# Channel attention as one pipeline of 36 pieces, with the next image's statistics in the scan

## The chip, the cores and the metric

The kernel runs on one core of a Trainium2 chip. Its time is the device time of one execution in microseconds (us), the median of three runs. The engines are TensorE (PE, with its weight loads as PEld), VectorE (DVE), ScalarE (ACT), GpSimd (POOL) and SyncE (SP), which issues the DMAs. All data are float32.

## The reference

Eight images of 384 channels and 64x64 pixels go through two layers, each added to its input. Layer 0 is attention over channels, layer 1 a selective scan over the pixels in four directions.

```python
x = x + conv_attention(gn(x))          # layer 0
x = x + selective_scan(gn(x))          # layer 1

gn(v): 32 groups of 12 channels; (v - mean) / sqrt(var + 1e-5) over group and pixels

conv_attention(x):
    q, k, v = [dwconv3x3(conv1x1(x, w), dw) for w, dw in ((wq, dwq), (wk, dwk), (wv, dwv))]
    q, k, v = split into 8 heads of 48 channels, each [48, 4096]
    q, k = q / |q|, k / |k|            # over the 4096 pixels
    attn = softmax(q @ k.T * temperature)          # [48, 48] a head
    return conv1x1(attn @ v, wproj)

selective_scan(x): for 4 orders of the 4096 pixels (rows, columns, both reversed)
    dt, B, C = projections of x        # per pixel: 384, 16 and 16 values
    for each pixel: h = h * exp(dt * A) + (dt * x) * B;  y = sum(h * C over 16) + D * x
    y of the 4 orders is summed; layer norm over channels; gelu
```

## The kernel before

Channels lie on partitions, as three blocks (`NJ`) of 128; an image is three tiles of 128x4096. Images go one after the other: `channel_attention(b)`, then `selective_scan(b)`. The finish of image b (layer norm, gelu, the addition, the store) is done within the attention of image b+1, and for the last image by `finish` at the end. Most order in the scan is pinned by `keep_in_program_order` (`pin`); the instructions of the attention were placed by a scheduler, from the order in which they are written.

*Attention.* `norm_factors` turns statistics (`bn_stats`, L162; `bn_aggr`, L118) into mean and inverse deviation of each group, with small matmuls against `avg` (L126, L138) and a Sqrt on ACT (L143). `weights` scales a 384x384 weight with it (L197) and makes the bias that replaces the mean (L201, L206). `conv` makes one block of 128 channels of k, q or v: 512 pixels at a time go through three matmuls (L226) into PSUM and with the bias on ACT into `pre` (L231). The 3x3 depthwise convolution follows: the centre tap is an ACT product (L236) or, with the taps above and below, three matmuls with diagonal weights (L249, copied by ACT at L254); all other taps are DVE operations `out = pre * w + out` (L266), over up to 64 rows each. `to_tokens` transposes k and q by PE (L290) with ACT copies (L291), `inverse_norm` squares and sums on ACT (L277), and L327 multiplies q and k over pixels. Masked softmax follows on DVE and ACT (L332 to L344), its result is multiplied into `wproj` (L362), and `project_out` applies that to v (L375), adds it to x (L380), takes the statistics for the second layer (L381) and stores x1. k and q go block by block over all rows, v in three stripes of rows. `token_norm` (L815, L816) takes the layer norm statistics of the last image at the start; `emit` places its 16 finish parts between the parts of v (L831, L838, L839, L843).

*Scan.* The second normalisation is applied in place (L438 on ACT for 6 of 24 blocks, L443 on DVE). Then 32 steps (4 orders by 8 chunks of 512 pixels) of 12 units (3 channel blocks by 4 groups of 4 states). A unit has four DVE scans (L586) of 512 pixels, four exponentials on ACT (L562), one POOL product of 128x2048 (L574), 16 PE transposes (L607), four ACT copies (L613) and 32 small products (L624). A step also has `step_size` (L528, L536, Softplus, with two table loads), `weigh` (L545), the layout of C (`mingle_c` on POOL L496, `turn_c` on PE L502, `spread_c` on DVE L513), and the loads of B (`fetch`, L519) from DRAM, where `lay_out` stored them. Results leave PSUM by DVE (L664, L666) and are added up in DRAM. In the last step `load_x` loads the next image into the tiles of x, and its 24 `bn_stats` blocks follow: one a unit after unit 5, and the rest behind the last scan.

All DMAs are issued by SP, in order. [...]

## Time and profile before

| | us |
|---|---|
| median of three runs | 19907.61 |
| lowest and highest | 19904.44, 19921.87 |
| the profiled execution's own time | 19929.61 |
| its span in the profile | 19927.8 |
| image 0: start to first scan | 488 |
| image 1: last scan of image 0 to its first scan | 490.4 |
| image 1: first to last scan | 1994.6 |
| last scan of image 7 to the end | 104 |

The mean granted PE clock is 0.949 of full speed. A row of the page gives line, engine, operation, output and inputs, count, busy time, mean duration in ns, and then how long the engine was idle before such instructions and what ended that. In a list in order of time, a row begins with start and length in us; several equal instructions are one row with their count (x8). Two instructions in a row overlap by some 0.1 us, as the next one starts before the last one's end is reported; so prices for a full queue are read from start to start. A float32 matmul is two instructions in this profile.

### The profile page before, as it was taken

The page shows a single profiled execution, that of the slowest core. Times are in us where ns is not written, and L with a number is a line of the kernel's source. Part 1 is how long each engine was busy: PE and PEld are TensorE (multiplying, and loading weights), DVE is VectorE, ACT ScalarE, POOL GpSimd, SP SyncE. Part 2 cuts the span into 40 slices and gives each one's busy share as a digit, 9 for nine tenths or more (in the row PEclk, how much of TensorE's full clock was granted, in tenths as well). Part 3 has the DMA queues.
Part 4 walks back from the last instruction along what each step waited for, and adds up shares of the span by engine and source line. Part 5 has one row for each costly group of instructions (what it writes and reads, how often), then busy time and mean ns, then how long its engine had stood idle before and what let it go on. Part 6 is the DMA issues. An engine that isn't in the chain of part 4 may idle for free. (4 is left out here: it accounts for less than half of the span.)

```text
span 19927.8 us, 414273 instructions
## 1 busy us (share of the span) xinstructions
PE 17323.4 (87%) x167376; PEld 10365.3 (52%) x167376; DVE 18841.2 (95%) x17078; ACT 16772.8 (84%) x29347; POOL 15425.1 (77%) x6798
## 2 busy tenths in 40 slices
PE   7888888888888888888888888888888888888887
PEld 4555545555455554555545555455554555545554
DVE  7999989999899998999989999899998999989998
ACT  3999949999499985999859998599985999859998
POOL 0999909999099980999819998199981999729997
PEclk9999989999899999999999999999999999999998
DMA  1232322323223232232322323223232222322223
GB/s 43 83 96 96 99 81 83 96 96 102 78 83 97 96 106 75 84 95 97 110 75 83 98 97 104 75 86 96 96 104 74 85 96 96 104 74 86 96 96 124
DMA packets 1194155, 1814.00 MB, mean 91 GB/s; under 512 B 153552, under 2 KB 1018064, under 8 KB 1055024
## 3 DMA queue, kind: packets, MB, share of 16 engines
q1 hardware_dynamic: 1191376, 1787.38, 27.5%
q8 instruction: 1321, 21.64, 0.4%
q14 instruction: 594, 4.87, 0.1%
q10 hardware_dynamic: 864, 0.12, 0.0%
HBM read 1468.39 MB, written 318.77 MB: 90 GB/s over the span
## 5 line engine op out<-in xcount | busy, mean ns | idle before, releaser
L574 POOL TENSOR_TENSOR db<-w,B 128x2048 f32<-128x2048 f32 x3072 | 14062.9, 4581 | 640.8 <-DVE h L586 428.9
L586 DVE TENSOR_TENSOR_SCAN h<-da,ca,db 128x512 f32<-128x512 f32 x10752 | 12785.7, 1266 | 285.0 <-ACT da L562 266.1
L562 ACT ACTIVATE da<-dt,neg_a 128x512 f32<-128x512 f32 x12288 | 8757.4, 714 | 156.4 <-DVE h L586 152.6
L607 PE MATMUL pt<-ident,h 128*128 128x128 f32 x49152 | 8091.3, 293 | 736.4 <-DVE h L586 468.7
L613 ACT COPY hc<-pt 128x512 f32<-128x512 f32 x12288 | 7411.5, 605 | 651.1 <-PE pt L607 590.1
L607 PEld LDWEIGHTS pt<-ident,h 128*128 128x128 f32 x49152 | 5420.5, 145 | 3192.8 <-issue 1892.3
L624 PE MATMUL py<-hc,cp 128*32 128x128 f32 x98304 | 5053.6, 289 | 898.6 <-ACT hc L613 726.3
L624 PEld LDWEIGHTS py<-hc,cp 128*32 128x32 f32 x98304 | 2039.4, 109 | 3163.9 <-ACT hc L613 1625.9
L423 POOL MEMSET wdt<- 128x1536 f32 x8 | 11.0, 1378 | 3564.8 <-DMA x1d<-x 3564.8
L586 DVE TENSOR_TENSOR_SCAN h<-da,db 128x512 f32<-128x512 f32 x1536 | 1747.7, 1209 | 83.4 <-ACT da L562 78.8
L474 PE MATMUL px<-x,wx 128*44 128x128 f32 x6144 | 1214.2, 341 | 50.2 <-ACT x L438 28.9
L545 POOL TENSOR_TENSOR w<-x,dt 128x512 f32<-128x512 f32 x744 | 1065.0, 1431 | 22.5 <-ACT dt L536 20.5
L474 PEld LDWEIGHTS px<-x,wx 128*44 128x44 f32 x6144 | 684.3, 127 | 378.6 <-issue 189.0
L528 PE MATMUL pd<-xd,wdt 128*128 128x512 f32 x1536 | 732.7, 613 | 157.9 <-DVE h L586 152.1
L513 DVE TENSOR_TENSOR cp<-quad,pct 128x512 f32<-128x512 f32 x1024 | 630.3, 683 | 44.9 <-PE pct L502 44.9
L375 PE MATMUL pp<-v,mT 128*128 128x512 f32 x1152 | 550.3, 631 | 117.2 <-DVE v L266 57.3
L600 POOL COPY ca<-h 128x4 f32<-128x4 f32 x2688 | 543.0, 202 | 0.0
L536 ACT ACT_TABLE_LOAD x256 | 328.4, 1283 | 229.3 <-PE pd L528 228.3
L528 PEld LDWEIGHTS pd<-xd,wdt 128*128 128x128 f32 x1536 | 272.5, 190 | 466.7 <-issue 238.2
L536 ACT ACTIVATE dt<-pd,dt_bias 128x512 f32<-128x512 f32 x768 | 475.7, 686 | 6.8 <-PE pd L528 2.2
L375 PEld LDWEIGHTS pp<-v,mT 128*128 128x128 f32 x1152 | 227.0, 203 | 394.7 <-issue 309.8
L666 DVE TENSOR_TENSOR ys<-ys,py 128x512 f32<-128x512 f32 x576 | 387.8, 673 | 4.3 <-PE py L624 4.3
(374 smaller groups left out, 10986.2 us busy)
## 6 DMA issues: line engine op xcount, KB each, us to landing
B<-bcd SPq DMA_DIRECT2D x1024, 1024.0 KB, 4.7
yd<-ys SPq DMA_DIRECT2D x384, 256.0 KB, 3.3
ys<-yd SPq DMA_DIRECT2D x768, 128.0 KB, 2.8
yd<-ys SPq DMA_DIRECT2D x768, 128.0 KB, 4.4
x<-in_x SPq DMA_DIRECT2D x48, 1024.0 KB, 5.5
x1d<-x SPq DMA_DIRECT2D x192, 256.0 KB, 2.0
ys<-yd SPq DMA_DIRECT2D x192, 256.0 KB, 2.9
fy<-yd SPq DMA_DIRECT2D x128, 384.0 KB, 3.8
```

Of the source, the lines that this page charges most:

```text
L375: nc.tensor.matmul(pc, lhsT=mT[:, j, bass.ts(m, P)], rhs=v[:, j, bass.ts(c, CH)], start=j == 0, stop=j == NJ - 1,)
L474: pin(nc.tensor.matmul(split(pxs[s][:XR, :])[:, part, :], lhsT=wx[:, j, k, :], rhs=view(x1[j], k, c)[:, part, :], start=i == 0, stop=i == ...
L513: pin(nc.vector.tensor_mul(t, m.broadcast_to([P, NQ, HP]), c.broadcast_to([P, NQ, HP])))
L528: pin(nc.tensor.matmul(pd, lhsT=wdt[:, k, bass.ts(j, P)], rhs=xds[s], start=True, stop=True))
L536: pin(nc.scalar.activation(dts[s, j], pd, AF.Softplus, bias=small["dt_bias"][:, j, k : k + 1]))
L545: pin(eng.tensor_mul(split(ws[s, j]), view(x1[j], k, c), split(dts[s, j])))
L562: pin(nc.scalar.activation(t, dts[s, j], AF.Exp, scale=neg_a[:, j, steps[s][0], n : n + 1]))
L574: pin(eng.tensor_mul(t, w.broadcast_to([P, NV, CH]), bts[s, g]))
L586: pin(nc.vector.tensor_tensor_scan(h, da, db, 0.0 if start else carries[s - 1][:, j, n : n + 1], ALU.mult, ALU.add,))
L607: pin(nc.tensor.transpose(t[:, f, :], hs[u][:, bass.ts(q, HP), :].rearrange("p l v -> p (l v)"), ident))
L613: pin(nc.scalar.copy(t, pts.pop((u, lb))))
L624: pin(nc.tensor.matmul(py[f * HP : (f + 1) * HP, lb, :], lhsT=cps[s, g][:, q, :], rhs=hc[:, f, :], start=g == lb == 0, stop=g == NG - 1 an ...
```

## The change

k, q and v are cut into 36 pieces of 16 rows (`PR`), first k and q block by block, then v with its three blocks in turn, and one loop over the pieces works at four of them at once: in step t, the 1x1 convolution of piece t+2 (`band`), the first products of piece t+1 (`start_sum`, `end_sum`), the closing of piece t (`finish_sum`), and, for k and q, transposes and squares of piece t-1 (`to_tokens`). All is pinned in this order.

The nine taps of a piece are split. ACT makes four products of 1024: one neighbouring row, left, right and centre. POOL adds left and right to the row's product. The centre goes to a PSUM tile of two banks (`ac`), DVE adds the five other taps to it there, and a last DVE addition joins both sums. No tap is a matmul now.

q's products with k, the norms and the softmax become steps of the loop; the roots are exp(-0.5 ln v) with one refinement. From step 27 on, projections and the finish of the last image run beside the pieces of v; its addition moves from DVE to POOL. The last image's layer norm statistics (`last_stats`) are read four parts ahead of the first piece and twelve parts during q.

The statistics of the next image move into the scan: `look_ahead` reads x a second time, in eight chunks of 128x3x512, takes their statistics in steps 29 to 31, and in the last step computes the norm factors, loads and scales the weight of k and makes its bias. At the start of the scan C's layout comes before the first products, ACT normalises three blocks before and nine after the first two decays, DVE twelve. `avg` is loaded once. The pools get `reuse_waits="tile"`.

```diff
+PR = 16
+NP = H // PR
+BR = CH // W
...
-def x_stats(x, stats, blocks):
-    for j, c in blocks:
-        tc.keep_in_program_order(
-            nc.vector.bn_stats(stats[:, j, c, :], x[j][:, bass.ts(c, CH)])
-        )
...
+while loaded:
+    i, y, x = loaded.pop(0)
+    pz = [bank(i, h) for h in range(2)]
+    for j in range(NJ):
+        for t in range(n):
+            pin(nc.tensor.transpose(
+                pz[j // 2][:, bass.ts((j % 2) * n + t, P)],
+                y[:, t * C + j * P : t * C + (j + 1) * P], ident,
+            ))
+    if loaded:
+        even(*loaded[0])
+    yield
+    cs, o = bass.ts(i, FT), y.rearrange("p (j l) -> p j l", l=FT)
+    for j in range(NJ):
+        pin(nc.scalar.activation(
+            o[:, j, :], pz[j // 2][:, (j % 2) * FT : (j % 2 + 1) * FT], AF.Gelu,
+            bias=small["ln_b"][:, j : j + 1], scale=small["ln_w"][:, j : j + 1],
+        ))
+    load_rest()
+    pin(nc.gpsimd.tensor_add(x, y, x))
+    load()
+    nc.sync.dma_start(
+        out_d[b, :, :, cs].rearrange("j p l -> p j l"), x.rearrange("p (j l) -> p j l", l=FT)
+    )
+    yield
...
-for tap in range(9):
-    if tap == 4:
-        continue
-    dy, dx = tap // 3 - 1, tap % 3 - 1
-    r0, r1 = max(y0, -dy), min(y1 if dx else ys, H - dy)
-    if r0 >= r1:
-        continue
-    x0, x1 = max(0, -dx), W - max(0, dx)
-    o = out3[:, r0 - y0 : r1 - y0, x0:x1]
-    nc.vector.scalar_tensor_tensor(
-        o, pre3[:, r0 + dy - lo : r1 + dy - lo, x0 + dx : x1 + dx],
-        dw[:, m, tap : tap + 1], o, ALU.mult, ALU.add,
-    )
...
-parts = (0, H // 2, 3 * H // 4, H)
-todo, left, edges = [], list(range(L // FT)) if emit else [], {}
-for y0, y1 in zip(parts, parts[1:]):
-    for m in range(NJ):
...
-        if m > 0:
-            for _ in range(min(len(todo), 6)):
-                project_out(*todo.pop(0))
-        for _ in range(min(len(left), 2)):
-            emit(left.pop(0))
-    todo += [(m, c) for c in range(y0 * W // CH, y1 * W // CH) for m in range(NJ)]
-for t in todo:
-    project_out(*t)
...
+work = st.enter_context(tc.tile_pool(name=f"a{b}", bufs=2, reuse_waits="tile"))
+ps_c = st.enter_context(tc.tile_pool(name=f"pc{b}", bufs=3, space=PSUM, reuse_waits="tile"))
+ps_s = st.enter_context(tc.tile_pool(name=f"ps{b}", bufs=2, space=PSUM, reuse_waits="tile"))
+ps_a = st.enter_context(tc.tile_pool(name=f"pa{b}", bufs=1, space=PSUM, reuse_waits="tile"))
...
+for j in range(NJ):
+    pin(nc.tensor.matmul(
+        pc[:, : n * W], lhsT=wts["w" + w][:, j, bass.ts(m, P)],
+        rhs=x[j][:, r * W : (r + n) * W], start=j == 0, stop=j == NJ - 1,
+    ))
+pin(nc.scalar.activation(
+    pre[:, o + r * W : o + (r + n) * W], pc[:, : n * W], AF.Identity,
+    bias=biases[w][:, m : m + 1],
+))
...
+def product(t, tap, dy, out=None):
+    pre, lo = rows_of(t)
+    y0 = PR * pieces[t][2] + dy - lo
+    if out is None:
+        out = work.tile([P, PR, W], F32, tag="pr", bufs=4, name=f"pr{b}_{t}_{tap}")
+    pin(nc.scalar.activation(out, pre[:, y0 : y0 + PR, :], AF.Copy, scale=weight(t, tap)))
+    return out
+def start_sum(t):
+    up = pieces[t][2] > 0
+    q, left = product(t, 1 if up else 7, -1 if up else 1), product(t, 3, 0)
+    pin(nc.gpsimd.tensor_add(q[:, :, 1:], q[:, :, 1:], left[:, :, : W - 1]))
+    sums[t] = q
+def end_sum(t):
+    q, right = sums[t], product(t, 5, 0)
+    pin(nc.gpsimd.tensor_add(q[:, :, : W - 1], q[:, :, : W - 1], right[:, :, 1:]))
+    accs[t] = ps_s.tile([P, PR, W], F32, tag="ac", name=f"ac{b}_{t}")
+    product(t, 4, 0, accs[t])
...
+def finish_sum(t, mid):
+    w, m, p = pieces[t]
+    pre, lo = rows_of(t)
+    y0, acc = PR * p, accs.pop(t)
+    for tap in (0, 2, 6, 8, 7 if y0 else 1):
+        mid(tap)
+        dy, dx = tap // 3 - 1, tap % 3 - 1
+        r0, r1 = max(y0, -dy), min(y0 + PR, H - dy)
+        x0, x1_ = max(0, -dx), W - max(0, dx)
+        o = acc[:, r0 - y0 : r1 - y0, x0:x1_]
+        pin(nc.vector.scalar_tensor_tensor(
+            o, pre[:, r0 + dy - lo : r1 + dy - lo, x0 + dx : x1_ + dx], weight(t, tap), o,
+            ALU.mult, ALU.add,
+        ))
+    out = out_of(t).rearrange("p (h w) -> p h w", w=W)
+    pin(nc.vector.tensor_add(out, acc, sums.pop(t)))
...
+def to_tokens(t, h):
+    w, m, p = pieces[t]
+    src = piece_out(t)[:, bass.ts(h, CH)]
+    pt = ps_c.tile([P, 4, P], F32, tag="pc", name=f"pt{b}_{t}_{h}")
+    for i in range(4):
+        pin(nc.tensor.transpose(pt[:, i, :], src[:, bass.ts(i, P)], ident))
+    n = 8 * p + 4 * h
+    if w == "k":
+        out = kT[:, n : n + 4, bass.ts(m, P)]
+    else:
+        out = qTs[t, h] = work.tile([P, 4, P], F32, tag="qT", name=f"qT{b}_{t}_{h}")
+    pin(nc.scalar.copy(out, pt))
+    i = m if w == "k" else NJ + m
+    pin(nc.scalar.activation(
+        src, src, AF.Square, accum_out=ssq[:, i, 2 * p + h : 2 * p + h + 1]
+    ))
...
+q = qTs.pop((t, h))
+for i in range(4):
+    n = 8 * p + 4 * h + i
+    pin(nc.tensor.matmul(
+        pas[m][:, : hi - lo], lhsT=q[:, i, :], rhs=kT[:, n, lo:hi],
+        start=n == 0, stop=n == NT - 1,
+    ))
...
+def norms():
+    polish_root(helper, roots, var)
+    rks = work.tile([P, 4, P], F32, tag="qT", name=f"rks{b}")
+    spread.append(rks.rearrange("p i l -> p (i l)"))
+    rks = spread[0]
+    for m in range(NJ):
+        r = rn[:, NJ + m : NJ + m + 1]
+        pin(nc.vector.tensor_mul(r, r, small["temp"][:, m : m + 1]))
+    for m in range(NJ):
+        pin(nc.vector.tensor_scalar_mul(rks[:, bass.ts(m, P)], ident, rn[:, m : m + 1]))
...
+def logits():
+    for m in range(NJ):
+        lo, hi = BANDS[m]
+        wd = hi - lo
+        lg = lgs[m] = ga[:, m, :]
+        pin(nc.vector.tensor_mul(lg[:, :wd], lg[:, :wd], spread[0][:, lo:hi]))
+        pin(nc.vector.scalar_tensor_tensor(
+            lg[:, :wd], lg[:, :wd], rn[:, NJ + m : NJ + m + 1], mask[:, m, :wd],
+            ALU.mult, ALU.add,
+        ))
+        mx = mxs[m] = tops[:, m : m + 1]
+        pin(nc.vector.reduce_max(mx, lg[:, :wd], axis=AX.X))
+        pin(nc.vector.tensor_scalar_mul(mx, mx, -1.0))
...
+def load_last(i):
+    if i == 0:
+        fin["mv"] = wp.tile([P, NT, 2], F32, name=f"fmv{b}")
+    y = work.tile([P, 2 * FT * NJ], F32, tag="acc", bufs=4, name=f"fs{b}_{i}")
+    y = y[:, : FT * NJ].rearrange("p (l c) -> p l c", c=C)
+    nc.sync.dma_start(y, before[2][bass.ts(i, FT), :].rearrange("(l p) c -> p l c", p=P))
+    fin["y"] = i, y
+def last_stats():
+    i, y = fin.pop("y")
+    n = FT // P
+    for t in range(n):
+        s = work.tile([P, nc.vector.BN_STATS_DIM], F32, tag="fst", name=f"fst{b}_{i}_{t}")
+        pin(nc.vector.bn_stats(s, y[:, t, :]))
+        pin(nc.vector.bn_aggr(fin["mv"][:, n * i + t, :], s))
...
+for t in range(-2, T):
+    ca, cb, cc, cd = t + 2, t + 1, t, t - 1
+    bs = bands(ca) if ca < T else []
...
+    elif t == KQ + 1:
+        guess_root(roots, var)
+    elif t == KQ + 2 and before:
+        last = finishing(before, parts, fin["of"], room, fin_bank, 4)
+        next(last)
+    elif t == KQ + 3:
+        ring[0] = 0
+        next(last, None)
+    def project():
+        if todo and fold_of:
+            ready.append(todo.pop(0))
+            project_in(*ready[-1])
+    def half(h):
+        if bs:
+            band(*bs.pop(0))
+        if grams:
+            gram(*grams.pop(0))
+        if 0 <= cb < T:
+            (start_sum, end_sum)[h](cb)
+        if turns:
+            to_tokens(cd, turns.pop(0))
+            grams.extend([(cd, h)] if pieces[cd][0] == "q" else [])
+        if t > KQ + 2:
+            next(last, None)
+            project()
+            next(last, None)
+    def mid(tap):
+        if tap == 2 and t == KQ + 1:
+            norms()
+        if tap == 2 and t == KQ + 2:
+            logits()
+        if tap in (2, 8) and ready and t > KQ + 3:
+            project_out(*ready.pop(0))
+    half(0)
+    if t == KQ + 3:
+        for j in range(NJ):
+            fold(j)
+    if t in (KQ + 1, KQ + 2):
+        finish_sum(cc, mid)
+    half(1)
+    for r in bs:
+        band(*r)
+    if t == KQ + 1:
+        spread_norms()
+    elif t == KQ + 2:
+        exponents()
+        shares()
+    project()
+    if t == KQ + 3:
+        project()
+    if stats_left and t < 0:
+        for _ in range(2):
+            load_last(stats_left.pop(0))
+            last_stats()
+    if 0 <= cc < T and t not in (KQ + 1, KQ + 2):
+        finish_sum(cc, mid)
+    while ready:
+        project_out(*ready.pop(0))
+    if t == KQ:
+        squares()
+    if "y" in fin:
+        last_stats()
+    if stats_left and NJ * NP - 1 <= cc:
+        load_last(stats_left.pop(0))
+    if 0 <= cc < T and pieces[cc][:2] == ("v", NJ - 1):
+        p = pieces[cc][2]
+        todo += [(m, c) for c in (2 * p, 2 * p + 1) for m in range(NJ)]
+for m, c in todo:
+    project_in(m, c)
+    project_out(m, c)
+    next(last, None)
+    next(last, None)
+all_of(last)
...
-    for c in range(NCH):
+    for c in range(5):
...
-            if c < 2:
+            if c < 1:
...
+mingle_c(0)
+turn_c(0)
+for g in range(NG):
+    spread_c(0, g)
 drive(0)
 drive(1)
 for i in range(2):
     decay(i)
-mingle_c(0)
-turn_c(0)
-for g in range(NG):
-    spread_c(0, g)
+for c in range(5, NCH):
+    for j in range(NJ):
+        s = x1[j][:, bass.ts(c, CH)]
+        pin(nc.scalar.activation(
+            s, s, AF.Identity, bias=shift[:, j : j + 1], scale=rstd[:, j : j + 1]
+        ))
...
+def look_ahead(u):
+    i = u - (U - 3 * UN)
+    if b + 1 == B or i < 0:
+        return
+    n, odd = divmod(i, 2)
+    if i == 0:
+        near["st"] = x_stats(b + 1)
+    if not odd and 1 <= n <= NCH:
+        for j in range(NJ):
+            pin(nc.vector.bn_stats(near["st"][:, j, n - 1, :], near["x"][:, j, :]))
+    if not odd and n < NCH:
+        near["x"] = big.tile([P, NJ, CH], F32, tag="near", name=f"nx{b}_{n}")
+        nc.sync.dma_start(
+            near["x"], x_d[b + 1, :, :, bass.ts(n, CH)].rearrange("j p l -> p j l")
+        )
+    if i == 2 * UN + 1:
+        near["f"] = norm_factors(big, ps_m, near["st"], f"0_{b + 1}", "m", pin)
+    if i > 2 * UN:
+        r = next(near["f"], None)
+        if r:
+            near["r"] = r
+    if i == 2 * UN:
+        near["w"] = load_wk(b + 1)
+    if i == 3 * UN - 2:
+        mean, rstd = near["r"]
+        scale_weights(near["w"], rstd)
+        bias = shift_of(big, ps_m, "m", near["w"], mean, f"{b + 1}k")
+        near["r"] += near["w"], bias
...
 for u in range(U + 1):
-    if u == U:
-        stats_next(4)
+    look_ahead(u)
     unit(u)
-    if u == U - UN + 5 and b + 1 < B:
+    if u == U - UN + 3 and b + 1 < B:
         x_next = load_x(b + 1)
-    if u >= U - UN + 6:
-        stats_next(1)
-stats_next(6)
...
-stats_next(len(blocks))
```

## The prediction

> **What bounds the kernel now.** I read the busy shares first, then a table of stretches for one whole image (image 1, from the last scan of image 0 to its own last scan), then the order of instructions in time inside the stretches, and last the waits of the scan.
>
> ```profile
> PE 17323.4 (87%) x167376; PEld 10365.3 (52%) x167376; DVE 18841.2 (95%) x17078; ACT 16772.8 (84%) x29347; POOL 15425.1 (77%) x6798
> 2483.00:2512.00 29.00, 15.71 (x104) 13.13 (x105) 14.34 (x31) 7.97 (x15) 1.06 (x1) 0.65 0.42 122
> 2512.00:2775.00 263.00, 227.84 (x834) 133.29 (x835) 229.68 (x169) 131.80 (x254) 0.00 (x0) 0.92 0.10 31
> 2775.00:2942.00 167.00, 142.97 (x406) 66.63 (x404) 151.85 (x141) 72.44 (x132) 1.56 (x2) 0.94 0.43 144
> 2942.00:2973.40 31.40, 10.09 (x51) 7.47 (x51) 16.31 (x35) 12.95 (x17) 8.43 (x5) 0.66 0.42 153
> 2973.40:4968.00 1994.60, 1771.30 (x19577) 1078.39 (x19577) 1947.16 (x1768) 1874.73 (x3255) 1917.07 (x843) 0.96 0.29 93
> ```
>
> The columns of a stretch are its length, then busy time of PE, weight load, DVE, ACT, POOL, then granted clock, DMA share, GB/s. 80% of an image is the scan (1994.6 us), where DVE is busy 98% and POOL 96%. The other 490 us are statistics and weights (29), k and q (263), v with output projection and the last image's finish (167), and the start of the scan (31). In k, q and v DVE is the busiest (230 of 263, 152 of 167), ACT is half idle and POOL does nothing. So the attention can be shortened and the scan can't, unless work leaves DVE and POOL there.
>
> ```profile
> 2917.24 10.23 DVE L266 SCALAR_TENSOR_TENSOR v<-pre1v,dwv,v 128x1008 f32<-128x1008 f32 x8 [1.59 <-ACT v L236]
> 2861.10 15.67 PE L375 MATMUL pp<-v,mT 128*128 128x512 f32 x36
> 2731.91 1.04 PE L290 MATMUL ptq<-ident,aq 128*128 128x128 f32 x8
> 2732.78 1.02 PE L226 MATMUL pc1q<-x,wq 128*128 128x512 f32 x2
> 2733.64 2.76 PE L327 MATMUL pa<-kT,qT 128*128 128x192 f32 x16
> 2736.24 1.04 PE L290 MATMUL ptq<-ident,aq 128*128 128x128 f32 x8
> 2781.31 1.18 ACT L236 ACTIVATE v<-pre1v,dwv 128x1024 f32<-128x1024 f32 x1
> 2782.35 0.89 ACT L366 COPY mT<-pmt 128x384 f32<-128x384 f32 x2
> 2555.36 0.67 ACT L231 ACTIVATE pre1k<-pc1k,bias1k 128x512 f32<-128x512 f32 x1
> 2555.93 0.57 ACT L291 COPY kT<-ptk 128x512 f32<-128x512 f32 x1
> 2556.39 0.64 ACT L277 ACTIVATE junkk<-ak 128x512 f32<-128x512 f32 x1
> 2556.93 0.20 ACT L277 ACTIVATION_READ_ACCUMULATOR junkk<-ak 128x1 f32 x1
> 2557.02 0.58 ACT L291 COPY kT<-ptk 128x512 f32<-128x512 f32 x1
> L574 POOL TENSOR_TENSOR db<-w,B x3072: 4492/4577/4748, 480.2 to 19809.8; 128x2048 f32<-128x2048 f32 x192
> L574 DVE TENSOR_TENSOR db<-w,B x8: 2292/2292/2293, 477.7 to 17827.2; 128x2048 f32<-128x2048 f32 x8
> L545 DVE TENSOR_TENSOR w<-x,dt x24: 691/692/694, 471.3 to 17822.8; 128x512 f32<-128x512 f32 x24
> L380 DVE TENSOR_TENSOR x<-x,pp 128x512 f32<-128x512 f32 x192 | 129.2, 684 | 41.7 <-PE pp L375 41.4
> POOL db L574 <- DVE h L586: 55.7, 37, 2.3
> DVE h L586 <- ACT da L562: 44.7, 106, 1.6
> ```
>
> These rows give prices from start to start, which count in a full queue. Eight taps of 1008, each adding to the same tile, take (10.23-1.27)/7 = 1.28 us apiece. A block of 512 columns through three 128x128 weights is 15.67/6 = 2.6 us of PE (a matmul is two instructions here), four transposes 0.87 (2731.91 to 2732.78), eight products of 192 columns 2.60, so 0.33 each (0.245 for 144 columns). On ACT 1024 elements cost 1.04, a block's bias 0.57, its transposed copy 0.46, its square with the sum 0.63.
>
> **The attention, part by part.** A piece is 16 rows of one of 9 row blocks (k, q, v by three).
>
> *One piece.* Eight DVE taps become five plus one closing addition: 6 x 1.28 = 7.7 us. ACT makes four products of 1024 (4.16), two biases (1.14) and, in k and q, two copies and two squares (2.2): 7.5 us. PE: two blocks 5.2, eight transposes 1.74, so 6.9 in k; with eight products (1.96 or 2.6) 8.9 or 9.5 in q, 9.1 on average. The tap matmuls (L249) go. POOL gets two additions of 1008: by L574's rate 2.25 us each, 4.5 a piece; the slowest w row (L545 on POOL reaches 1719 ns for 512) would make it 3.4 and 6.8. Both ends stay under 7.7, so POOL costs nothing while DVE is the cover; if DVE were faster than 6.8 it could show.
>
> [...] By the row of the stretch, POOL is idle for 263 us, and its slower additions lie beside the taps. I follow the row.
>
> [...] The sum now lies in PSUM, where no DVE row here writes. [...] The nearest rows, L380 (one PSUM input, 684 ns) and L545 (none, 692), show no surcharge. I take 1.28; the lower end is the overlapped 1.2, the upper end open to 1.7 since each tap reads what the last one wrote there.
>
> *The sum.* E is the end of the last scan, 2482.9. PE is free at E+5 (last copies at 2487), does three blocks (7.7), ACT two and a half biases and four products (about 6); DVE's first tap could start at E+20. But the first four parts' statistics of the old image now stand ahead of it on DVE, and they wait for y's last store and a load (3 to 4 us each by the DMA list) plus 4 x 1.3: I take E+24. dwk's load stands on SP behind y's last store and lands near E+12, before ACT needs it. Table loads in the attention fall from seven an image to three, on an ACT that is half idle: nothing. Then
> - 13 steps bound by DVE's taps: 7.7 plus 0.5 for hand-over = 8.2: 107.
> - 12 q steps bound by PE: 9.1 plus 0.6 = 9.7: 116. The other statistics (1.3 a step) hide here: 7.7+1.3 = 9.0.
> - v: two steps carry norms and softmax on DVE (7.7+2.4, and 7.7+3+1.3 with a wait for ACT's Exp): 23. One folds the projection (4.5) and projects three blocks: 16. Four with two blocks, three projections and two finish parts on PE (5.2+7.7+2.6 = 15.5): 62. Two bound by ACT (5.3 and two parts at 2.6): 21. The last two 18, the tail of six projections 15.5 on PE, 18 with a slow restart as in L375's 12.63 us for four blocks. With 3 for hand-over 161.
>
> That ends at E+408. Before, the last statistic ends at 2941.7 = E+458.8. Gain 51 us an image. Image 0 has no finish (25 us less in v) and no old statistics, but its first taps start at 50 as before: 410 against 456.8, gain 47.
>
> *Start of the scan.* The C work (L496, L502, L513) moves ahead of the first products. Now POOL does it after 4.5 us of L574, so DVE waits 5.6 us at 2971. Its input should land before B's 2963.15, so I take 6 us of gain. Nine of the normalisations go behind ACT's first decays; they lie in the wait for B, about 5 us long, and would cost up to 5 us if it shrank.
>
> *Inside the scan.* 24 statistics at 0.6 start to start = 14.4 us join DVE in images 0 to 6, of which 5 (3 us) were there: +11.4, as DVE has only 45 us of slack in 1995 and POOL is within 2% of it too. bn_aggr and six small operations add 1.5. Sqrt brings two table loads of 1.28 and the weights' scaling 1.6 on ACT, which runs three decays ahead: 1 of that shows. Statistics of one block come in threes, after which ACT and POOL have caught up: -2. Total +12. The eight loads of 768 KB wait on SP until the chunk before is used, and ahead of B and y transfers; B is fetched four units (20 us) early, so nothing. They add 44 MB to 1814 at a DMA share of 0.29. x's own load moves two units earlier, ahead of one y store, and lands long before E either way.
>
> *Total.* Images 1 to 6: 51+6-12 = 45; image 7 57; image 0 41; together 368 us. The profiled execution ran 19929.6 us with a span of 19927.8, 22 us over the median shown, 19907.6. Span after 19560; median 19540.
>
> **Rivals.**
> 1. *A denser pipeline.* No hand-over loss (0.5 us over 36 pieces, 18 us), and statistics that fit into the slack (10): 26 us an image more, 19,330. For it: four engines with work for others in hand; against: every engine has a fixed order.
> 2. *A looser one.* Fixed order makes ACT, PE and DVE wait in turn, or the clock is 0.92 as in the k and q stretch, which alone makes q's 9.1 into 9.9. 0.8 us a piece is 29 us an image, 19,770. The wait list of before is full of such turns.
> 3. *Slower: taps in PSUM.* If a dependent tap there takes 1.75 us, not 1.28, a piece takes DVE 10.5: +2.3 on 13 steps, +2.1 on 12, and 11 us in v, 66 us an image, so 20,070. It decides from about 1.6 us on. For it: no row writes PSUM from DVE, and all six operations of a piece form one dependent chain; against: L380.
> 4. *No change*: losses of 2 and a scan that gives back 25 us rather than 12.
>
> **How the numbers follow.** Likeliest 0.50, 19,540 (alone 19,430 to 19,680); denser 0.18; looser 0.18; slower 0.09; no change 0.05. A measurement of this kernel tells 0.2%, 40 us, from none. Faster 0.86, same 0.05, slower 0.09. The range 19,300 to 19,830 takes in denser and looser and leaves out the slow case and the ends.
>
> **What would show it.** Right: DVE taps on ac near 1.28 us; one image from last scan to first scan near 434 us, not 490; k steps near 8, q steps near 9.7; POOL's additions at 2.3 us with no wait behind them; scan stretches of 2007 us in images 0 to 6. Wrong: taps over 1.6 us, POOL's addition over 3.8, DVE waiting for ACT products in k, or a scan over 2020.

## The result, and the profile after

The changed kernel takes 19575.5 us (median of 4 runs, 19568.9 to 19593.0), against 19906.0 us of the kernel before on the same chip: a ratio of 0.9836, 95% interval 0.9819 to 0.9853. Run once more with the experiments' kernels it took 19572.2 us, ratio 0.9825 (0.9812 to 0.9839). The forecast was 19540. The total is close to it, but its two main terms are not: the attention got shorter by more than forecast, and the scan got longer by more.

The busy shares of the profiled execution (span 19591.2 us) show what moved. VectorE has 388 us less than before, ScalarE 811 and POOL 1449 us more:

```profile
PE 17097.0 (87%) x166560; PEld 10219.2 (52%) x166560; DVE 18453.4 (94%) x17510; ACT 17584.1 (90%) x30011; POOL 16874.4 (86%) x7486
```

Next the table of stretches for image 1, cut at what DVE does: from the last scan of image 0 to the first tap, k, q, v up to the last sums, the start of the scan, the scan. The columns are those of the table before.

```profile
2461.70:2482.20 20.50, 20.20 (x94) 9.86 (x95) 5.73 (x17) 10.01 (x14) 2.79 (x2) 1.00 0.53 164
2482.20:2578.40 96.20, 81.75 (x249) 38.95 (x247) 89.28 (x75) 89.06 (x140) 53.15 (x25) 0.95 0.02 5
2578.40:2687.10 108.70, 100.75 (x446) 64.67 (x447) 104.58 (x125) 95.73 (x153) 52.38 (x25) 1.00 0.19 58
2687.10:2852.00 164.90, 138.45 (x391) 66.14 (x390) 127.54 (x150) 109.83 (x168) 76.51 (x38) 0.91 0.44 140
2852.00:2880.80 28.80, 17.15 (x75) 11.62 (x73) 17.44 (x36) 13.70 (x19) 2.69 (x4) 0.83 0.45 155
2880.80:4898.05 2017.25, 1782.37 (x19569) 1088.93 (x19569) 1961.55 (x1789) 1880.19 (x3261) 1925.24 (x845) 0.96 0.30 96
```

In k and q all four engines now have work side by side, DVE busy 93 and 96% of the stretch. In v it has 37 us without work. The scan is 2017 us, where it was 1991 (the stretch shown before ran 4 us past its last scan).

For all images I read the start of the first scan and the end of the last one from DVE's instructions in time, for every kernel of this study in the same way. The last three steps, where `look_ahead` works, run from the start of the 1393rd of an image's 1536 scans to the end of the last one; this column is a mean of images 0 to 6 too:

| kernel | us, ratio to before with interval | scan, mean of images 0 to 6 | its last three steps | scan, image 7 | last scan to next first scan, mean | first scan of image 0 |
|---|---|---|---|---|---|---|
| before | 19906.0 | 1988.2 | 184.9 | 1986.5 | 490.3 | 487.9 |
| changed | 19575.5, 0.9836 (0.9819 to 0.9853) | 2018.6 | 211.9 | 1988.3 | 418.2 | 442.1 |
| changed, again | 19572.2, 0.9825 (0.9812 to 0.9839) | 2017.1 | 212.2 | 1987.9 | 418.4 | 437.9 |
| a_undo | 19588.4, 0.9829 (0.9816 to 0.9843) | 1990.7 | 182.1 | 1989.2 | 447.3 | 440.0 |
| a_nostats | 19527.3, 0.9799 (0.9785 to 0.9812) | 2010.0 | 202.7 | 1987.5 | 417.5 | 441.3 |
| a_lock | 19555.7 (one run) | 2014.0 | 205.0 | 1989.4 | 418.1 | 437.5 |
| a_tail | 19536.7, 0.9803 (0.9790 to 0.9817) | 2010.1 | 203.5 | 1989.3 | 418.1 | 437.7 |
| a_both | 19449.9, 0.9763 (0.9735 to 0.9791) | 2000.9 | 194.9 | 1986.1 | 418.5 | 438.6 |
| p_sbuf | 20057.8, 1.0071 (1.0054 to 1.0088) | 2017.4 | 212.2 | 1992.5 | 477.9 | 487.4 |
| p_dve | 20253.4, 1.0169 (1.0153 to 1.0184) | 2015.2 | 211.7 | 1986.8 | 502.9 | 527.4 |
| p_both | 20405.0, 1.0245 (1.0224 to 1.0265) | 2015.7 | 211.9 | 1988.8 | 525.5 | 524.3 |
| c_order | 19627.1, 0.9854 (0.9840 to 0.9869) | 2016.5 | 211.8 | 1983.2 | 425.6 | 448.5 |
| best | 19442.3, 0.9763 (0.9749 to 0.9776) | 1994.9 | 189.9 | 1985.3 | 420.3 | 444.7 |
| best2 | 19468.0, 0.9777 (0.9764 to 0.9791) | 1993.4 | 184.6 | 1992.6 | 427.9 | 449.2 |

The changed kernel's row accounts for the span: seven times 72.1 us of attention and 45.8 us in image 0 are 551 us gained; seven scans longer by 30.4 us and 2 us in image 7 are 215 us lost; the difference is 336, and the spans differ by 336.6 us. One kernel's scans scatter by some 4 us, so a mean over seven is good to about 2 us. This scatter lies in the first 29 steps, for which the kernels have means of 1803 to 1809 us. The last three steps scatter by no more than 1.5 us, so below I compare these, with 212.0 us, the mean of the changed kernel's two profiles. In image 7 they take 181 to 183 us in every kernel and on each of the chips used. Image 7 has no next image, and its scan is as long as before. So the whole loss of the scan comes with what was put into it for the next image's sake, and 27 of the 30 us are lost in the last three steps; the other 3 are within the scatter of the first 29.

### The profile page after: what moved, and what is told of

It is laid out like the page before. It is cut to its first block, busy times and chain, and to the rows that moved or that the text cites. A ratio compares the mean times of both kernels' runs of the same rounds, so it can differ in the third digit from the quotient of the medians.

```text
span 19591.2 us, 415258 instructions
## 1 busy us (share of the span) xinstructions
PE 17097.0 (87%) x166560; PEld 10219.2 (52%) x166560; DVE 18453.4 (94%) x17510; ACT 17584.1 (90%) x30011; POOL 16874.4 (86%) x7486
## 4 chain that ended last, share of the span: by engine, by line
ACT 27%; PE 23%; DVE 15%; issue 4%; POOL 3%; DMA 1%; SPq 0%; DVEq 0%; ACTq 0%; POOLq 0%
ACT da L898 12%; ACT hc L949 10%; PE pt L943 10%; DVE h L922 10%; PE py L960 5%; PE px L810 3%; DVE ac L451 3%; POOL db L910 2%; ACT dt L872 1%; PE pp L599 1%; PE pd L864 1%; PE py L966 1%; ACT pr L413 1%; ACT L872 1%; ACT L898 1%
## 5 line engine op out<-in xcount | busy, mean ns | idle before, releaser
L420 POOL TENSOR_TENSOR pr<-pr,pr 128x1008 f32<-128x1008 f32 x288 | 673.3, 2338 | 1201.1 <-ACT pr L413 1184.0
L426 POOL TENSOR_TENSOR pr<-pr,pr 128x1008 f32<-128x1008 f32 x288 | 574.8, 1996 | 277.2 <-ACT pr L413 193.8
```

The lines of the kernel that those rows point to most:

```text
L420: pin(nc.gpsimd.tensor_add(q[:, :, 1:], q[:, :, 1:], left[:, :, : W - 1]))
```

## The experiments

The edits are cut to what matters; `...` marks a gap, and comments in them are mine.

### What the scan pays for the next image's statistics

At the end of image 0's scan, the changed kernel's DVE and POOL show two of the small operations of the variance taking far more than their 0.16 us:

```profile
2399.36 2.43 DVE L922 TENSOR_TENSOR_SCAN h<-da,ca,db 128x512 f32<-128x512 f32 x2
2401.71 0.13 DVE L154 COPY mean<-pm 128x3 f32<-128x3 f32 x1
2401.88 1.08 DVE L155 TENSOR_TENSOR var<-mv,mean 128x3 f32<-128x3 f32 x1
2402.99 4.42 DVE L156 TENSOR_TENSOR var<-var 128x3 f32<-128x3 f32 x1
2407.45 0.16 DVE L157 TENSOR_TENSOR var<-var,mv 128x3 f32<-128x3 f32 x1
```

```profile
2398.38 9.02 POOL L910 TENSOR_TENSOR db<-w,B 128x2048 f32<-128x2048 f32 x2
```

POOL's two products begin at 2398.38 and take 4.5 us each. L155 ends with the first of them, at 2402.96; L156 ends with the second: at 2407.41, POOL's at 2407.40. Both read two tensors in SBUF. In all seven scans L155 and L156 together take 5.5 to 6.5 us, and the wait ends with POOL's second product; in three of them L155 alone is held through the rest of the first product and the whole second one, 5.7 to 6.4 us, as in image 2's scan:

```profile
7275.77 5.74 DVE L155 TENSOR_TENSOR var<-mv,mean 128x3 f32<-128x3 f32 x1
```

```profile
7272.47 9.02 POOL L910 TENSOR_TENSOR db<-w,B 128x2048 f32<-128x2048 f32 x2
```

The scans between read one operand in PSUM (`da`) and one in SBUF, and do not stop: the two from 2399.36 take 2.43 us beside the product, and one takes 1.263 us on average over the run. Two more stops stand a little later: a scan behind the table loads of the Sqrt on ACT, and the bias behind its matmuls on PE.

```profile
2429.17 2.46 DVE L922 TENSOR_TENSOR_SCAN h<-da,ca,db 128x512 f32<-128x512 f32 x2 [2.61 <-ACT da L898]
2451.48 0.16 DVE L274 TENSOR_SCALAR bias1k<-pb1k 128x3 f32<-128x3 f32 x1 [4.99 <-PE pb1k L269]
```

The Sqrt sits between two table loads of 1.28 us on ACT, which makes `da`. My theory was that some 14 us of the loss are such stops and some 15 the statistics themselves. The rivals were the additional loads and some after-effect of the new attention. Four kernels were run for it.

**a_lock**: the variance with one SBUF tensor an operation and scalar operands.

```diff
-        pin(nc.vector.tensor_sub(var, mv[:, :, 0], mean))
-        pin(nc.vector.tensor_mul(var, var, var))
-        pin(nc.vector.tensor_add(var, var, mv[:, :, 1]))
+        for j in range(NJ):
+            d = var[:, j : j + 1]
+            pin(nc.vector.tensor_scalar(d, mv[:, j, 0:1], mean[:, j : j + 1], None, ALU.subtract))
+            pin(nc.vector.tensor_scalar(d, d, d, mv[:, j, 1:2], ALU.mult, ALU.add))
```

> Only the first of those edits: the small variance operations read one tensor in SBUF, with scalar operands, instead of two. Theory A (an operation of VectorE on two SBUF tensors stands still while POOL's product of 4.6 us runs): in each scan the group of 1.08 and 4.42 us becomes six operations of under 0.2 us each, and the scans are 5 us shorter on average, 2013. Theory B (those operations were slow for another reason, such as the row of the statistics before them): single ones still take over 1 us.

The last three steps fell by 7.0 us (the whole scans by 3.9, in one profile), where theory A had 5. The six operations in DVE's list, and POOL's products at that time:

```profile
2396.92 0.21 DVE L157 TENSOR_SCALAR var<-mv,mean 128x1 f32<-128x1 f32 x1
2397.17 0.27 DVE L158 TENSOR_SCALAR var<-var,mv 128x1 f32<-128x1 f32 x1
...
2398.04 0.27 DVE L158 TENSOR_SCALAR var<-var,mv 128x1 f32<-128x1 f32 x1
2398.23 4.80 DVE L923 TENSOR_TENSOR_SCAN h<-da,ca,db 128x512 f32<-128x512 f32 x4
```

```profile
2393.57 9.10 POOL L911 TENSOR_TENSOR db<-w,B 128x2048 f32<-128x2048 f32 x2
```

POOL's products run all the while, and none of these six takes over 0.27 us; in the rows of a_tail, a_both and best, which have the same edit, none takes over 0.28. With scalar operands in SBUF the operations did not stop. The edit changes the kind of operation together with the second tensor; the closing additions below (L456), of the old kind but with one operand in PSUM, take 1.225 us beside POOL as without it (p_dve), so here it is the second SBUF tensor that counts.

**a_tail**: that, and the bias taken from PSUM two units after its matmuls were issued.

```diff
                 if i == 3 * UN - 2:
                     mean, rstd = near["r"]
                     scale_weights(near["w"], rstd)
-                    bias = shift_of(big, ps_m, "m", near["w"], mean, f"{b + 1}k")
-                    near["r"] += near["w"], bias
+                    near["b"] = shift_in_two(big, ps_m, "m", near["w"], mean, f"{b + 1}k")
+                    next(near["b"])                  # the matmuls
+                if i == 3 * UN:
+                    near["r"] += near["w"], next(near["b"])   # the bias on DVE
```

> Two edits at the end of the statistics only: the variance of the three blocks is made by operations with one tensor in SBUF and scalar operands (instead of two tensors in SBUF), and the bias is taken from PSUM one unit after its matmuls were issued. Theory A (VectorE is held up there: 5.5 us at the two-operand operations by POOL's running product, 5 us by the wait for the bias' matmuls): the stalls vanish and the scans of images 0 to 6 fall by 10 us to about 2008, time 19505. Theory B (what VectorE waits for there is late anyway, and the wait moves to the next scan, which needs POOL's product and ACT's decay): scans within 3 us of 2018.7, time within 25 us of 19575.

The last three steps fell by 8.5 us (the whole scans by 7.8): theory A, somewhat less than its 10. But a_lock alone had 7.0 of it. Taking the bias later brought 1.5 us and not the 5 of its wait, as theory B says of such stops: most of that wait was made up afterwards.

**a_nostats**: 21 of the 24 statistics left out.

```diff
                 if not odd and 1 <= n <= NCH:
-                    for j in range(NJ):
-                        pin(nc.vector.bn_stats(near["st"][:, j, n - 1, :], near["x"][:, j, :]))
+                    if n == 1:
+                        for j in range(NJ):
+                            pin(nc.vector.bn_stats(near["st"][:, j, 0, :], near["x"][:, j, :]))
+                        for m in range(1, NCH):
+                            pin(nc.gpsimd.tensor_copy(near["st"][:, :, m, :], near["st"][:, :, 0, :]))
```

> Left out: 21 of the 24 statistics operations of the next image's x inside the scan; the three of the first 512 columns are made and copied by POOL for the other seven blocks. Loads, factors, weights and bias stay where they are. Theory A (statistics about 15 us, the small operations' stalls about 14 us an image): scan stretches of images 0 to 6 fall by 13 us from 2018.7 to about 2006, time 19485. Theory B (the loads' transfers cost, not the operations): scans stay at 2015 to 2020, time within 30 us of 19575. Theory C (the statistics cost all of it, by delaying ACT and POOL behind them): scans near 1990, time 19375.

They fell by 9.3 us (the whole scans by 7.9), not 13: the 21 operations need some 12.6 us of DVE at about 0.6 us from start to start, so about 3 us of them lay in time that the scan has over. This is nearest to theory A, outside B's 2015 to 2020, and contradicts C.

**a_both**: a_tail and a_nostats in one, to see whether the two gains add. It was run last, after `best` below had gained more than the single edits promised.

> Left out: 21 of the 24 statistics of the next image's x inside the scan, as in the run that left them out alone; and the two edits that took the stalls at the scan's end away. The loads of x stay in the scan. It tells why the best version's scans fell to 1994.9 us, 22 below the changed kernel's 2017.1, where the two single edits had given 8.6 and 8.5. Theory A (the loads of 6.3 MB and their waits cost the other 5): scans of images 0 to 6 at 2000 to 2002. Theory B (statistics and stalls cover each other: with either one gone ACT and POOL catch up less, and both must go): scans at 1994 to 1997.

They do: 17.1 us against 9.3 and 8.5, and theory A's 2000 to 2002 for whole scans holds. What is left above the 182.1 of the next kernel, which has nothing of all this in its scan, is 12.8 us. The kernels `best` and best2 below part it further. `best` has the loads and all statistics elsewhere and takes 189.9, so the loads, three statistics and POOL's copies cost 5.0. best2 has aggregation, averages and Sqrt elsewhere too and takes 184.6, so these cost some 5; 2.5 are left for loading and scaling `wk` and for its bias.

**a_undo**: the statistics, factors, scaling and bias at the start of the next attention again, with `x` loaded whole as before; the pipeline stays. The new function does for every image what the changed kernel did ahead of image 0, and `look_ahead` returns at once.

```diff
+    def prepare(b, x):
+        st0, wk = x_stats(b), load_wk(b)
+        for j in range(NJ):
+            for c in range(NCH):
+                pin(nc.vector.bn_stats(st0[:, j, c, :], x[j][:, bass.ts(c, CH)]))
...
     for b in range(B):
+        x = prepare(b, x[0])
         x1, x1_d, stats1 = channel_attention(b, *x, before)
```

> Undone: the statistics of the next image's x, its factors, the scaling of wk and the bias go from the scan to the start of that image's attention, as they were before the change; the pipeline over 36 pieces stays. Theory A (the scan pays about 30 us an image for them: 15 for the statistics themselves on a full VectorE and 14 for stalls of the small operations at its end): scan stretches of images 0 to 6 fall from 2018.7 us on average to 1988 as in image 7; the first tap moves from 20.5 us after the last scan to about 36 (29 us as in the old start, 3 for the five statistics that were in the scan even then, 4 for the four parts of the old image); net 15 us an image, 105 in all: 19470. Theory B (the scan is longer for another reason, such as x's extra loads or a slower granted clock in the attention before it): the scans stay above 2010 and the time rises by some 80 us to 19650.

The scans came back to 1990.7, near the 1988 of theory A, but the attention grew by 29 us, not by the 15.5 I had worked out, and the time is that of the changed kernel. DVE at the start of image 1:

```profile
2435.16 14.33 DVE L1226 BATCH_NORM_STATS2 st<-x 128x6 f32<-128x512 f32 x24
2449.41 0.81 DVE L150 BATCH_NORM_AGGREGATE mv<-st 128x2 f32<-128x48 f32 x3
...
2462.63 0.16 DVE L274 TENSOR_SCALAR bias1k<-pb1k 128x3 f32<-128x3 f32 x1 [4.90 <-PE pb1k L269]
...
2480.47 2.45 DVE L451 SCALAR_TENSOR_TENSOR ac<-pre1k,dwk,ac 128x945 f32<-128x945 f32 x2 [12.37 <-ACT ac L413]
```

```profile
2462.85 19.46 PE L364 MATMUL pc1k<-x,wk 128*128 128x512 f32 x41 [0.25 <-DVE bias1k L274]
```

The last scan ends at 2430.2. The bias is there at +32.4, and only then can PE and ACT begin with the blocks and products that a piece needs before its first tap, which comes at +50.2, where the changed kernel has it at +20.5. I had put that lead of 18 us beside the statistics; it stands behind them. So moving the statistics ahead is worth 29 us an image at the start of the attention, and in the form it has in this change it costs as much in the scan.

### The sum in PSUM, and POOL's additions

The forecast's slower case was that a tap whose sum lies in PSUM takes longer. The taps in the changed kernel take 1.27 us, and POOL's additions and the closing addition are near their forecasts of 2.25 and 1.28:

```profile
L420 POOL TENSOR_TENSOR pr<-pr,pr 128x1008 f32<-128x1008 f32 x288 | 673.3, 2338 | 1201.1 <-ACT pr L413 1184.0 <-DMA fy<-x1d 16.0 <-DMA x1d<-x 1.0
L426 POOL TENSOR_TENSOR pr<-pr,pr 128x1008 f32<-128x1008 f32 x288 | 574.8, 1996 | 277.2 <-ACT pr L413 193.8 <-DVE ac L451 63.9 <-DMA fy<-x1d 15.2
L456 DVE TENSOR_TENSOR acc<-ac,pr 128x1024 f32<-128x1024 f32 x192 | 235.2, 1225 | 25.5 <-DVE ac L451 1.0 <-PE pc7q L364 0.5 <-PE pb3q L269 0.5
```

Three kernels and the changed one form a square: the sum in PSUM or (in half of the pieces) in SBUF, the additions on POOL or on DVE.

**p_sbuf**:

```diff
+            def in_sbuf(t):
+                return 0 < t < 10 or t > KQ + 2
             def end_sum(t):
...
-                accs[t] = ps_s.tile([P, PR, W], F32, tag="ac", name=f"ac{b}_{t}")
+                if in_sbuf(t):
+                    accs[t] = out_of(t).rearrange("p (h w) -> p h w", w=W)
+                else:
+                    accs[t] = ps_s.tile([P, PR, W], F32, tag="ac", name=f"ac{b}_{t}")
```

> For nine of the twelve k pieces (the second to the tenth) and the last nine v pieces of every image the sum of taps lies in SBUF (in the piece's own output buffer) instead of PSUM, so that each tap and the closing addition read two SBUF tensors; the other half of the pieces stays in PSUM. POOL goes on making its two additions. Theory A (a VectorE operation on two SBUF tensors and POOL's addition exclude each other): a k step takes up to 7.6 + 4.3 = 11.9 us instead of 8.0, taps show 2 to 3.5 us where POOL adds, and 72 k and 72 v pieces make the run 250 to 450 us longer, 19850 to 20050. Theory B (the place of the sum does not matter, or PSUM is the dearer place): taps stay at 1.27 us, k steps at 8.0, time within 40 us of 19600.

The attention grew by 59.6 us an image, 3.3 for each of the 18 pieces. The run is some 485 us longer than the changed kernel's, a little over theory A's 250 to 450, and slower than before. DVE and POOL in a stretch of k in which ACT's products come unevenly:

```profile
2542.61 10.06 DVE L457 SCALAR_TENSOR_TENSOR acc<-pre1k,dwk,acc 128x1008 f32<-128x1008 f32 x5
2552.78 3.28 DVE L462 TENSOR_TENSOR acc<-acc,pr 128x1024 f32<-128x1024 f32 x1
2555.99 6.29 DVE L457 SCALAR_TENSOR_TENSOR acc<-pre1k,dwk,acc 128x1008 f32<-128x1008 f32 x5
2562.38 1.23 DVE L462 TENSOR_TENSOR acc<-acc,pr 128x1024 f32<-128x1024 f32 x1
```

```profile
2544.33 3.04 POOL L420 TENSOR_TENSOR pr<-pr,pr 128x1008 f32<-128x1008 f32 x1 [2.72 <-ACT pr L413]
2547.94 2.34 POOL L429 TENSOR_TENSOR pr<-pr,pr 128x1008 f32<-128x1008 f32 x1 [0.58 <-ACT pr L413]
2552.66 2.32 POOL L420 TENSOR_TENSOR pr<-pr,pr 128x1008 f32<-128x1008 f32 x1 [2.37 <-ACT pr L413]
2563.90 2.00 POOL L429 TENSOR_TENSOR pr<-pr,pr 128x1008 f32<-128x1008 f32 x1 [8.92 <-ACT pr L413]
```

The five taps from 2542.61 have two POOL additions within them and take 10.06 us; the closing addition behind them meets a third and takes 3.28. The five taps from 2555.99, with POOL silent, take 6.29, and their closing addition 1.23. That is theory A.

**p_dve**: POOL's additions on DVE, between the taps of the piece before.

```diff
-                pin(nc.gpsimd.tensor_add(q[:, :, 1:], q[:, :, 1:], left[:, :, : W - 1]))
+                adds.append((t, q[:, :, 1:], left[:, :, : W - 1]))
...
-                pin(nc.gpsimd.tensor_add(q[:, :, : W - 1], q[:, :, : W - 1], right[:, :, 1:]))
+                adds.append((t, q[:, :, : W - 1], right[:, :, 1:]))
...
                 for tap in (0, 2, 6, 8, 7 if y0 else 1):
                     mid(tap)
+                    if adds and tap in (2, 8):
+                        add_one()                  # nc.vector.tensor_add
```

> POOL's two additions of every piece go to VectorE (between the taps of the piece before), the sum of taps stays in PSUM. By the rows (an addition of 1008 takes VectorE some 1.25 us, POOL 2.0 to 2.3 us beside it): a k step grows from 8.0 to 10.5 us, a q step from 9.06 to 11.5, a v piece by up to 2.5; 75 us an image, 20150 to 20200. [...]

```profile
L420 DVE TENSOR_TENSOR pr<-pr,pr 128x1008 f32<-128x1008 f32 x576 | 700.2, 1216 | 320.4 <-ACT pr L413 318.5
```

The attention grew by 84.6 us an image; the rows had said 75. By stages, the means of images 1 to 7 grew by some 46 us in k, 30 in q and 7 in v, which has 37 us to spare. An addition takes DVE 1.22 us, where POOL takes 2.0 to 2.3, and DVE waits 318 us in the run for ACT's products at the place where I put the additions, though it waits 134 us less for PE in v. An order with fewer such waits might cost less than 84.6 us. By an estimate from these rows it could hardly cost under 47: of the 72 additions an image, 48 fall to k and q and are 58 us of DVE, where the changed kernel has 11 us without work.

**p_both**: both edits together.

> Both edits at once: additions on VectorE, and half of the sums in SBUF. Theory A (the price of SBUF sums is the exclusion with POOL): with POOL silent, the taps on two SBUF tensors take 1.27 us, and the run is as long as with the additions alone on VectorE, within 40 us. Theory B (two SBUF operands cost VectorE more by themselves): it is longer than that by as much as the SBUF sums cost with POOL at work. [...]

It is 152 us longer than p_dve, so the expectation of equal times failed, and by its wording theory B should hold. The groups of taps show what happens; `pre0` is image 0, and `pre1` image 1:

```profile
L467 DVE SCALAR_TENSOR_TENSOR v<-pre0v,dwv,v 128x1008 f32<-128x1008 f32 x30 | 37.8, 1262 | 0.2
L467 DVE SCALAR_TENSOR_TENSOR v<-pre1v,dwv,v 128x1008 f32<-128x1008 f32 x30 | 50.4, 1680 | 0.2
L467 DVE SCALAR_TENSOR_TENSOR acc<-pre1k,dwk,acc 128x1008 f32<-128x1008 f32 x28 | 35.4, 1264 | 0.2
```

In k the SBUF taps take 1.264 us, in v of image 0 1.262, but in v of images 1 to 7 1.680. There POOL is not silent: the finish of the image before has its 16 additions of 128x768 (L249) in exactly that stretch, and image 0 has no finish. POOL is held up as well: beside the same SBUF sums in p_sbuf these additions take 2.39 us on average, and 1.82 in the changed kernel. In v of image 3, against p_dve, the taps take 14 us more (only those of 1008 and 945 elements are longer), the additions moved to DVE, which read two SBUF tensors too, 3.5 and the closing additions 1.6. That is 19 of the 21 us by which this v is longer; the attention grew by 22.6. In image 0 the first scan came 3 us earlier than in p_dve. So theory A stands, and the error was mine: I had overlooked POOL's other additions when I called it silent. Without POOL the place of the sum made no difference: in k of image 1 a tap on an SBUF sum takes 1.264 us, and one with its sum in PSUM 1.268.

### The order at the start of the scan

**c_order**: the C work behind the first two products again.

```diff
-            mingle_c(0)
-            turn_c(0)
-            for g in range(NG):
-                spread_c(0, g)
             drive(0)
             drive(1)
+            mingle_c(0)
+            turn_c(0)
+            for g in range(NG):
+                spread_c(0, g)
```

> Undone: at the start of each scan POOL's copy of C and the spreading of C come after the first two products again, as before the change. Theory A (the first scan waits for C behind POOL's 4.5 us product): the stretch from the last scan of one image to the first of the next grows from 418.2 us by 5 to 8, 48 us in all, 19650 on this chip. Theory B (what the first scan waits for is B's transfer, about 3 us before C is ready): under 2 us an image, time within 20 us of 19600.

The stretch between scans is 7.3 us longer: theory A. DVE at the start of image 1's scan, first in c_order, then in the changed kernel:

```profile
2875.43 2.29 DVE L910 TENSOR_TENSOR db<-w,B 128x2048 f32<-128x2048 f32 x1 [4.16 <-DMA B<-bcd]
2883.25 2.48 DVE L849 TENSOR_TENSOR cp<-quad,pct 128x512 f32<-128x512 f32 x4 [5.53 <-PE pct L838]
2885.65 2.33 DVE L922 TENSOR_TENSOR_SCAN h<-da,db 128x512 f32<-128x512 f32 x2
```

```profile
2875.71 2.48 DVE L849 TENSOR_TENSOR cp<-quad,pct 128x512 f32<-128x512 f32 x4 [1.57 <-PE pct L838]
2878.32 2.29 DVE L910 TENSOR_TENSOR db<-w,B 128x2048 f32<-128x2048 f32 x1
2880.80 2.34 DVE L922 TENSOR_TENSOR_SCAN h<-da,db 128x512 f32<-128x512 f32 x2 [0.19 <-DMA B<-bcd]
```

The wait of 5.53 us for C is gone, and the spreading fills the wait for B's transfer.

### A version that uses what was found

In v the changed kernel's DVE waits for PE's projections, and a statistic takes some 0.6 us. So **best** puts the next image's statistics there, one ahead of each sum of x and projection, loaded into buffers that are free in v, and keeps a_tail's edits.

```diff
             def project_out(m, c):
+                stat_ahead()      # bn_stats of the next 128x512 of x[b + 1], then the load after the next
                 s = x[m][:, bass.ts(c, CH)]
                 pin(nc.vector.tensor_add(s, s, pps.pop((m, c))))
```

> The statistics of the next image's x go from the scan into the v part of the image before, one in front of each sum of x and projection, where VectorE waits for TensorE's projections (259 us in the run); factors, weights and bias stay in the scan, with the two edits that took VectorE's stalls away there. Theory A (in v VectorE has idle time in front of those sums, 32 us an image for 16 us of statistics): scans of images 0 to 6 at 2001 us (2018.6 less 8.6 for the statistics and 8.5 for the stalls), attention 418 to 422, the run 100 us shorter than the changed kernel on the same chip. Theory B (VectorE and TensorE alternate in v, so each statistic in front of a sum delays the next projection's bank): attention longer by 10 us or more, the run at most 50 us shorter.

```profile
L606 DVE TENSOR_TENSOR x<-x,pp 128x512 f32<-128x512 f32 x192 | 131.6, 685 | 259.1 <-PE pp L599 259.1
```

```profile
L633 DVE TENSOR_TENSOR x<-x,pp 128x512 f32<-128x512 f32 x192 | 131.0, 682 | 181.8 <-PE pp L604 181.8
```

The first row is the changed kernel's, the second that of best: the wait for PE falls from 259.1 to 181.8 us, and the attention grows by only 2 us an image. The scans fall to 1994.9. The run takes 19442.3 us (19436.0 to 19452.1), beside 19572.2 us (19555.6 to 19579.8) of the changed kernel on the same chip: 130 us less, more than theory A's 100. It is the fastest kernel of this study, at 0.9763 of before.

**best2** moves the factors out of the scan too: their averages between the last projections of v, and their Sqrt next to that of the scan's own factors. For this all 24 statistics must be done earlier, so two stand in front of each of the first twelve sums.

```diff
+            left = 5 if b + 1 < B else 0
             for m, c in todo:
                 project_in(m, c)
                 project_out(m, c)
+                if left:
+                    next(ahead["f"])      # aggregation, averages, variance of the next image
+                    left -= 1
...
-                mean, rstd = all_of(norm_factors(np_, ps_t, stats1, f"1_{b}", "t", pin))
+                steps1 = norm_factors(np_, ps_t, stats1, f"1_{b}", "t", pin)
+                for _ in range(6):
+                    next(steps1)
+                if next_factors:
+                    next(next_factors)    # its Sqrt
+                mean, rstd = next(steps1)
```

> As the one before, and the factors leave the scan too: two statistics stand at each of the first twelve sums of v, the averages are made between the last projections, and the square root stands next to that of the scan's own factors, so that no table is loaded for it inside the scan; only wk's scaling and the bias stay there. Theory A (what is left of the scan's loss is these operations and two table loads of 1.28 us): scans at 1992 us, attention 420 to 425, 130 to 150 us shorter than the changed kernel. Theory B (the chain of factors delays the end of the attention as much as it did the scan): attention at 430 or more, no shorter than the one before.

The last three steps are some 5 us shorter than in best; over the whole scan 1.5 us of it are left, as the first 29 steps, alike in both kernels, came out 3.8 us longer, within their scatter. The attention is 7.6 us longer, at 427.9 us between theory A's 425 and theory B's 430, and at 19468.0 us the run is slower than best. From v's first tap to its last, images 1 to 6 take 6.2 us more than in best, and from there to the last statistic of x1 3.6 us more. In the first of these parts best2 has six statistics more, in the second it has the factors instead. So the chain of factors is at most a part of the loss; how much the doubled statistics cost was not tried alone.

The repeated run of the changed kernel, for comparison, came out as expected, at 0.9825, 2017.1 and 418.4:

> The changed kernel itself once more, beside the next two and on their chip, to compare them with it: 0.983 to 0.985 of before, scans of images 0 to 6 2018 us, from the last scan of an image to the first of the next 418 us.

## Why the forecast was right, and where it was not

*Bound and mechanism: right in k.* In k the step is DVE's, busy 93% of it, as forecast. Twelve k steps took 96.2 us, 8.0 each (forecast 8.2).

*q: PE's term was too large.* I had 9.7 us a step, bound by PE at 9.1 with 0.6 of hand-over; it is 9.06 (108.7/12). PE's busy time there is 100.75/12 = 8.4. A matmul of float32 is two instructions in the profile (before's L375 has 1152 for eight images of 72), but a transpose is one: before's L290 has 768 for k, which are eight images of 96 transposes. So the row that I read as four transposes in 0.87 us holds eight. In the changed kernel's q:

```profile
2616.32 1.14 PE L488 MATMUL pa<-kT,qT 128*128 128x144 f32 x8
2617.30 0.60 PE L467 MATMUL pt<-ident,acc 128*128 128x128 f32 x4
2617.74 2.74 PE L364 MATMUL pc1q<-x,wq 128*128 128x512 f32 x6
2620.32 1.14 PE L488 MATMUL pa<-kT,qT 128*128 128x144 f32 x8
```

Four products take 0.98, four transposes 0.44, a block 2.58: only the transposes differ from my prices. With eight at 0.87 instead of 1.74, 9.1 becomes 8.2. The granted clock is not the reason; where I read these prices in before, it was 1.00, as it is in q now (the columns are those of the stretches):

```profile
2731.20:2738.00 6.80, 6.80 (x43) 5.80 (x42) 5.20 (x7) 4.56 (x11) 0.00 (x0) 1.00 0.01 2
2861.10:2876.60 15.50, 15.50 (x38) 6.85 (x38) 13.91 (x16) 4.33 (x9) 0.00 (x0) 1.00 0.51 172
```

So DVE with its taps and the old image's statistics, which I had priced at 9.0, is the bound, busy 96%. Image 0, which has no such statistics, takes 101.0 us for q, 8.4 a step, and there PE is busy 95% and DVE 89%. In images 1 to 7 the twelve steps make 7.7 us less than forecast.

*v: right in its sum.* 170.3 us to the last statistic, at 2857.4, against 161 and one DVE-bound step of 8.2, which I had counted with k. DVE waits for PE in the steps with projections, as forecast. The single terms were off both ways, and that the sum fits is in part luck: the folding step took 19.6 us instead of 16, and a finish part's transposes had the double price of q's.

*The start: 20.5 us against 24*; the statistics of the old image wait for their load as forecast, which is there at 15.2 us, and the first tap follows 5 us behind it. *The scan's start: 8 us gained instead of 6*, confirmed by c_order at 7.3. These terms together make the gain of images 1 to 7 72 us where I had 57.

*Image 0 gained less, 45.8 us against 53.* Its v, from 252.5 us to the last statistic at 416.0, takes 163.6 us, little less than image 1's 170.3: I had taken off 25 us for the finish that it lacks, and the finish costs v only 7. Its first tap came at 55 us instead of 50; q, 15 us under its forecast, made up for most of this.

*The scan: the step that failed.* I forecast +12 us an image and it is +30. I had 11.4 for statistics and 2.5 for all else, less 2 that ACT and POOL were to catch up. By the last three steps, the 21 statistics cost 9, about what I had; the small operations of the variance, held by POOL, 7; the wait for the bias 1.5; the loads, which I had at nothing, 5 with the few operations beside them; aggregation, averages and Sqrt 5; and `wk` with its bias 2.5. So "all else" is some 20 us and not 2.5. I had named Sqrt's loads and the small operations. What I had not seen is that a small operation on DVE would be held by one or two POOL products of 4.5 us, here for 4.4 to 6.4 us, while the scans stand behind it in the queue.

*The place of the sum.* I had taken 1.28 us for a tap whose sum lies in PSUM, and it takes 1.27. With POOL silent a tap of 1008 on an SBUF sum takes 1.262 us (image 0 of p_both) and one on a PSUM sum 1.267 (p_dve), 5 ns apart. The rival built on dear taps in PSUM had the sign of the place wrong: a sum in SBUF is the dear one here, as long as POOL adds beside it (1.680 us a tap in v of images 1 to 7 of p_both).

*POOL's additions.* POOL took 2.34 and 2.00 us where DVE takes 1.22 (p_dve); moving them to DVE cost 84.6 us an image all the same. But that a slower engine was free here was only half of the reason. The split paid in full because the sum lies in PSUM: with half of the sums in SBUF, the attention lost 60 us again.

So the total, 337 us of span against 368 forecast, is close by luck: it holds two errors that nearly cancel, 99 us too little for the attention's gain and 131 us too little for the scan's loss.

## What to carry to other kernels

When POOL works beside VectorE, as here, let every VectorE operation there have at most one tensor in SBUF: put the running sum into PSUM (here five taps of 1008 took 10.06 us on an SBUF sum with POOL adding, 6.29 with POOL silent), or use scalar operands for small vectors (0.27 us instead of 4.42). Check what a row's count stands for in the program before taking a price from it. Before moving work out of one stage, price it as what it displaces in the other stage's fullest queue, small operations and their waits included, and look first for a stage in which that engine waits for another one, as VectorE does for TensorE in v (259.1 us in the run). A move that frees the start of a pipeline is worth the statistics and the lead of the pipeline behind them, here 29 us rather than 15.
